# A planned RWKV block on one core: the landing times in the planner made later, and the turns of all pieces of work listed anew

## The chip, the cores and the metric

The kernel runs on one core of a Trainium2 chip. The metric is the device time of one execution in microseconds (us); lower is better. The kernel before was timed three times: 614.04, 616.27 and 617.69 us, with a median of 616.27 us.

## What is computed

The reference is one RWKV block with eight sequences of 256 tokens, 512 channels and 32 heads of 16 channels. Cut to what matters:

```python
xn = ln(x, ln1_w, ln1_b);  sx = token_shift(xn, state[:, 1])
xxx = tanh((xn + sx * maa_x) @ maa_w1).reshape(b, l, 5, 1, 32)
x5 = xn[:, :, None] + sx[:, :, None] * (maa_stack + matmul(xxx, maa_w2))
w = exp(-exp(time_decay + tanh(x5[:, :, 1] @ decay_w1) @ decay_w2))
r, k, v = x5[3] @ Wr.T, x5[0] @ Wk.T, x5[2] @ Wv.T
g = silu(x5[4] @ Wg.T)
# for every token t, with s a 16x16 state per head:
#   a = k_t v_t^T;  out_t = r_t (u * a + s);  s = a + w_t * s
att = group_norm(outs) * gn_w + gn_b
x = x + att * g @ Wo.T
xn2 = ln(x, ln2_w, ln2_b);  sx2 = token_shift(xn2, state[:, 0])
rr = sigmoid((xn2 + sx2 * ffn_maa_r) @ ffn_Wr.T)
kk = square(relu((xn2 + sx2 * ffn_maa_k) @ ffn_Wk.T))
x = x + rr * (kk @ ffn_Wv.T)
```

Everything is in 32-bit floats.

## The kernel before

**Stages.** The work of each of the eight sequences ("batches" b = 0 to 7) is cut into three stages: `inputs_of_scan` (first norm, token shift, the five mixes, the projections k, v, r, g and the decay w), `scan` (the recurrence), and `rest` (group norm, output projection Wo, second norm, and the feed-forward part with the weights Wfk, Wfr and Wfv). Constants and the weights Wk, Wr, Wg and Wv stay in SBUF. Wo, Wfk, Wfr and Wfv are loaded again for each batch, each in two halves of 512 KB, into a pool of four tiles called `Ws`. At any time the stages of three neighbouring batches overlap: the rest of one, the scan of the next, the inputs of the one after.

**The scan.** A batch has four channel blocks of four row groups, so 16 pieces of scan for a batch and 128 in all. For each piece v must stand repeated over 16 rows. To get that, v is first written to a DRAM tile `vo` by a DMA of ScalarE's queue, and then read back by a DMA of SyncE's queue that broadcasts it into a tile `vs` of 512 KB (six such tiles). A broadcast for batch b, block and row group is called vs*b*_*block*_*group* below. When it has landed, a small ScalarE copy (L944) sets the start value, a VectorE multiply (L951, in six pieces a GpSimd one, L948) brings in k, VectorE scans (L953), GpSimd multiplies by r (L956), and TensorE sums over the rows (L964).

**The planner.** No piece is issued where it is written. Each call adds a piece of work (`Op`) to a `Plan`: its engine, a cost, the tiles it writes and reads. There are 2648 pieces: 400 of TensorE, 490 of VectorE, 1102 of ScalarE, 405 of GpSimd, 251 DMAs of SyncE's queue. `TURNS` gives each piece a number from 0 to 2647, its turn, in 25 rows: one for the constants and one for each of the 24 stages, and within a row in the order in which the pieces were added. `order` then takes again and again, of the pieces whose inputs have all been placed, the one with the lowest turn, gives it a start in a calendar of its own, and puts it off if no tile of a pool that it needs is free. So the turns fix the order of the instructions on each engine, and on SyncE's queue the order of the DMAs. That queue works in order: a DMA whose tile is not yet free holds up all DMAs behind it.

**The landing times.** In that calendar a transfer lands `WAY` (1.4 us) plus a wire time after its start, and its user may start a further lag later. Both numbers come from `LANDS`, by the name of the tile; what has no entry gets (KB / 308, 1.7). Transfers also share the wire: one lands no sooner than the one before it plus its own wire time. The calendar has one more effect on the program: where several tiles of a pool are free, a piece gets the one that by the calendar came free last. Nothing else of the calendar is in the program; engines and queues wait for semaphores alone.

Of the kernel before, what the change touches and what calls it, by code (L numbers as in the profile page):

```python
# [68 lines left out]
class Plan:  # L69
# [5 lines left out]
    LANDS = {"vs__": (2.3, 1.45), "rsb_": (0.5, 0.5), "sq_": (0.5, 0.5), "s": (0.3, 1.4), "vo_": (0.7, 1.4), "vo__": (0.35, 1.4),  # L75
             "o_": (0.7, 1.2), "x": (1.8, 1.3), "xt": (1.7, 1.3), "xs": (0.7, 0.9), "idt": (0.2, 1.6)}
# [43 lines left out]
    def stage(self):  # L120
# [1072 lines left out]
```

## Time and profile before

| | |
|---|---|
| median of three timed runs | 616.27 us |
| the profiled execution's own time | 617.54 us |
| its span, first to last instruction | 615.8 us |
| median issue to landing: broadcasts `vs`, 128 of them | 5.8 us |
| the same: Wo, Wfk, Wfr, Wfv halves, 16 each | 5.8, 7.0, 5.9, 5.0 us |
| the same: x for the residual, x for the first norm | 6.3, 6.1 us |
| the same: state, v written to DRAM, output | 5.1, 5.1, 4.6 us |
| ScalarE table loads | 36 of 1.28 us |

The profiled execution took 1.3 us more than the median of the timed runs. In the profile PE is TensorE's matmuls, PEld its weight loads, DVE VectorE, ACT ScalarE, POOL GpSimd, SP SyncE. "L951" is line 951 of the kernel. A wait "DVE vs L951 <- DMA vs<-vo" is time in which VectorE stood idle before an instruction of line 951 that writes a `vs` tile, until a DMA from `vo` to `vs` had landed. The matmuls of this kernel all have line 432, 826, 964 or a few others, since a helper issues them. Ends of matmuls are modelled, so that a busy PE is not a PE at its peak.

### The profile page before, as it was taken

The numbers are of one execution on the slowest core, as the hardware profiler recorded it, in microseconds if no ns is written. First come the engines' busy times: TensorE is split into PE (matmuls) and PEld (weight loads), VectorE is DVE, ScalarE is ACT, GpSimd is POOL, SyncE is SP. The second block draws the span as 40 slices with busy tenths as digits, with TensorE's granted clock in tenths as the row PEclk, the third lists the DMA queues.
The fourth block names the chain that finished last, engine by engine and source line by source line (L and its number), as shares of the span: only waits on it lengthen the run. The fifth ranks groups of instructions, "written<-read, shape, count | busy, mean of one in ns | idle before, by whom it ended". The sixth has DMA issues, their size and how long they took to land.

```text
span 615.8 us, 17481 instructions
## 1 busy us (share of the span) xinstructions
PE 599.6 (97%) x7246; PEld 349.9 (57%) x7246; DVE 543.5 (88%) x492; ACT 508.5 (83%) x1166; POOL 520.1 (84%) x417
## 2 busy tenths in 40 slices
PE   8999999899999999998999999999999999999987
PEld 7575555467544864376553674455644564556464
DVE  5799899999999997898989998999999999995342
ACT  5988689989999999976999888998988789955341
POOL 2899999999999998998879997999979997987030
PEclk9999999999999999999999999999999999999999
DMA  9798784788959677659688896876967599781632
GB/s 310 217 251 224 205 199 140 201 212 224 243 145 264 162 200 218 179 155 246 183 240 247 221 255 166 213 187 172 259 180 229 134 267 255 208 228 32 224 124 81
DMA packets 52639, 124.76 MB, mean 203 GB/s; under 512 B 5840, under 2 KB 11344, under 8 KB 52560
## 3 DMA queue, kind: packets, MB, share of 16 engines
q1 hardware_dynamic: 48048, 119.39, 70.3%
q10 hardware_dynamic: 4512, 4.26, 2.2%
q8 instruction: 57, 0.93, 0.7%
q14 instruction: 22, 0.18, 0.1%
HBM read 115.25 MB, written 8.39 MB: 201 GB/s over the span
## 4 chain that ended last, share of the span: by engine, by line
PE 56%; POOL 15%; ACT 14%; DVE 5%; DMA 5%; issue 4%; ACTq 0%; DVEq 0%; POOLq 0%
PE ps L432 46%; POOL st L956 8%; DMA vs<-vo 5%; PE ps L964 5%; POOL mix L786 2%; PE ps L644 2%; PE ps L826 2%; POOL mix L700 2%; ACT L1117 1%; DVE st L953 1%; ACT mix L698 1%; ACT sq L1023 1%; ACT ps L768 1%; ACT wrep L932 1%; PE ps L555 1%
## 5 line engine op out<-in xcount | busy, mean ns | idle before, releaser
L953 DVE TENSOR_TENSOR_SCAN st<-wrep,vs 128x1024 f32<-128x1024 f32 x128 | 288.9, 2278 | 4.6 <-PE ps L964 1.1
L956 POOL TENSOR_TENSOR st<-st,r 128x1024 f32<-128x1024 f32 x128 | 254.5, 2004 | 10.9 <-DVE st L953 10.7
L951 DVE TENSOR_TENSOR vs<-vs,ps 128x1020 f32<-128x1020 f32 x122 | 143.0, 1203 | 8.4 <-DMA vs<-vo 7.8
L432 PE MATMUL ps<-Ws,mix 128*32 128x512 f32 (+3 forms) x872 | 115.7, 586 | 0.4 <-DVE o L1084 0.2
L432 PEld LDWEIGHTS ps<-Ws,mix 128*32 128x32 f32 (+1 forms) x872 | 38.4, 116 | 62.7 <-issue 52.1
L700 POOL TENSOR_TENSOR mix<-mix,xn 128x512 f32<-128x512 f32 x44 | 47.7, 1099 | 29.1 <-DVE mix L693 22.8
L786 POOL TENSOR_TENSOR mix<-mix,xn 128x512 f32<-128x512 f32 x62 | 66.9, 1098 | 6.1 <-DVE mix L770 5.8
L964 PE MATMUL ps<-st,con 128*32 128x256 f32 x1024 | 62.6, 380 | 0.5 <-POOL st L956 0.3
L432 PE MATMUL ps<-mix,Wv 128*32 128x256 f32 (+1 forms) x856 | 59.8, 379 | 1.5 <-DVE mix L783 1.0
L432 PE MATMUL ps<-mix,Wg 128*32 128x256 f32 (+1 forms) x664 | 58.6, 380 | 2.6 <-ACT w L849 1.7
L432 PE MATMUL ps<-mix,Wr 128*32 128x256 f32 (+1 forms) x832 | 59.2, 380 | 0.0
L432 PE MATMUL ps<-mix,Wk 128*32 128x256 f32 (+1 forms) x760 | 59.0, 379 | 0.0
L432 PE MATMUL ps<-mix,Ws 128*32 128x256 f32 (+1 forms) x664 | 57.5, 379 | 1.4 <-DVE mix L693 1.4
L432 PE MATMUL ps<-Ws,g 128*32 128x512 f32 (+1 forms) x416 | 57.1, 593 | 1.5 <-POOL g L1035 1.5
L912 ACT COPY att<-ps 32x256 f32<-32x256 f32 x128 | 46.6, 364 | 4.9 <-PE ps L904 1.6
L432 PEld LDWEIGHTS ps<-mix,Wg 128*32 128x32 f32 (+1 forms) x664 | 40.5, 124 | 17.6 <-issue 2.5
L768 ACT ACTIVATE ps<-ps,vec 128x256 f32<-128x256 f32 x112 | 46.6, 444 | 4.3 <-PE ps L432 3.0
L432 PEld LDWEIGHTS ps<-mix,Ws 128*32 128x32 f32 (+1 forms) x664 | 40.0, 124 | 17.2 <-DVE mix L693 1.8
L432 PEld LDWEIGHTS ps<-mix,Wv 128*32 128x32 f32 (+1 forms) x856 | 38.6, 115 | 18.7 <-DVE mix L783 1.4
L432 PEld LDWEIGHTS ps<-mix,Wk 128*32 128x32 f32 (+1 forms) x760 | 39.3, 119 | 17.4 <-issue 1.5
L964 PEld LDWEIGHTS ps<-st,con 128*32 128x32 f32 x1024 | 33.2, 110 | 28.0 <-issue 5.1
L432 PEld LDWEIGHTS ps<-mix,Wr 128*32 128x32 f32 (+1 forms) x832 | 36.7, 116 | 19.5 <-issue 2.0
(134 smaller groups left out, 962.4 us busy)
## 6 DMA issues: line engine op xcount, KB each, us to landing
vs<-vo SPq DMA_DIRECT2D x128, 512.0 KB, 5.8
Ws<-in_wo SPq DMA_DIRECT2D x16, 512.0 KB, 5.8
Ws<-in_fk SPq DMA_DIRECT2D x16, 512.0 KB, 7.0
Ws<-in_fr SPq DMA_DIRECT2D x16, 512.0 KB, 5.9
Ws<-in_fv SPq DMA_DIRECT2D x16, 512.0 KB, 5.0
x<-in_x SPq DMA_DIRECT2D x9, 512.0 KB, 6.3
vo<-v ACTq DMA_DIRECT2D x15, 256.0 KB, 5.1
out<-o SPq DMA_DIRECT2D x15, 256.0 KB, 4.6
```

The source lines that it names most:

```text
L432: nc.tensor.matmul(out[i : i + n], lhsT=w[:, i : i + n], rhs=x, start=first, stop=final)
L555: nc.tensor.matmul(ps()[:, 0, :], lhsT=warm[:, 0, 0:P], rhs=warm[:, 0, 0:T], start=True, stop=True)
L644: nc.tensor.transpose(to[:, m, n * P : (n + 1) * P], xh[n]()[:, k * P : (k + 1) * P], idt())
L700: gp(512, t, [t, xn[q]], lambda q=q, t=t: nc.gpsimd.tensor_tensor(t(), t(), xn[q]()[:, :, 1 : T + 1], ALU.add))
L768: act(256, p_, [p_, vec], lambda g=g, q=q, m=m, p_=p_: nc.scalar.activation(p_()[:, m, :], p_()[:, m, :], AF.Identity, bias=col(f"maa_{g}" ...
L786: gp(512, t, [t, xn[q]], lambda q=q, t=t: nc.gpsimd.tensor_tensor(t(), t(), xn[q]()[:, :, 1 : T + 1], ALU.add))
L826: nc.tensor.matmul(pd()[i : i + 32, 0, :], lhsT=w, rhs=src[k // 2]()[:, k % 2, :], start=(k == begin), stop=(k == end))
L912: act(350, atts[q], [pc], lambda i=32 * (2 * q + m), m=m, q=q, h=32 * h: nc.scalar.copy(atts[q]()[h : h + 32, m, :], pc()[i : i + 32, 0, :]))
L951: dve(4 * T, [vs], [vs, kp], lambda m=m, vs=vs, kp=kp: nc.vector.tensor_tensor(vs()[:, :, 1:T], vs()[:, :, 1:T], kp()[:, m : m + 1, 1:T].t ...
L953: dve(4 * T, [st], [w, vs, first], lambda w=w, vs=vs, st=st: nc.vector.tensor_tensor_scan(st().rearrange("p n t -> p (n t)"), w().rearrang ...
L956: gp(4 * T, st, [st, r], lambda m=m, st=st, r=r: nc.gpsimd.tensor_tensor(st(), st(), r()[:, m : m + 1, :].to_broadcast([P, 4, T]), ALU.mul ...
L964: nc.tensor.matmul(pat()[32 * i : 32 * i + 32, 0, :], lhsT=con()[:, s : s + 32], rhs=done[i]()[:, j, :], start=(j == 0), stop=(j == 3),)
```

## The change

It does two things. In `LANDS` the second number (the lag) of most transfers grows, and the four streamed weights get entries of their own:

```diff
-    LANDS = {"vs__": (2.3, 1.45), "rsb_": (0.5, 0.5), "sq_": (0.5, 0.5), "s": (0.3, 1.4), "vo_": (0.7, 1.4), "vo__": (0.35, 1.4),
-             "o_": (0.7, 1.2), "x": (1.8, 1.3), "xt": (1.7, 1.3), "xs": (0.7, 0.9), "idt": (0.2, 1.6)}
+    LANDS = {"vs__": (2.3, 2.45), "s": (0.3, 2.4), "vo_": (0.7, 2.2), "vo__": (0.35, 2.0), "o_": (0.7, 1.2), "x": (1.8, 2.3),
+             "xt": (1.7, 2.0), "xs": (0.7, 0.9), "idt": (0.2, 1.6), "Wfk_": (1.7, 2.7), "Wfr_": (1.7, 2.7),
+             "Wfv_": (1.7, 2.7), "Wo_": (1.7, 2.7)}
```

No DMA of this kernel has a tile named `rsb` or `sq` first, so the two entries that go meant nothing. And all 25 rows of `TURNS` are new:

```diff
     TURNS = """
-        8 74 18 43 53 81 61 64 90 79 102 99 173 150 5 33 118 145 151 146 24 15 34 26 47 49 31 46 56 30 35 48 32
-        44 60,
...
+        14 20 12 17 19 82 83 21 23 93 134 116 107 106 3 35 110 121 146 168 9 10 13 49 50 51 34 56 61 48 53 54 47
+        55 59,
...
```

The first row shows how such a row is read. Its places 11 and 12 are the two halves of Wr (from 102 and 99 to 134 and 116), places 13 and 14 those of Wg (from 173 and 150 to 107 and 106). Read in the same way, some DMAs that are spoken of below, with their turns before and after, and in brackets how many turns their first user comes behind them:

| DMA | before | after |
|---|---|---|
| vs0_2_3 | 286 (1) | 275 (14) |
| vs0_2_1 | 308 (1) | 271 (38) |
| xt3 and x20, x for later stages | 279, 266 | 410, 313 |
| vs4_0_1 | 1308 (25) | 1320 (32) |
| vs4_0_3 | 1328 (29) | 1304 (8) |
| vs4_0_2 | 1345 (13) | 1324 (38) |
| Wfr2, the two halves | 1267, 1317 | 1263, 1276 |
| Wfk2, the two halves | 1306, 1356 | 1307, 1225 |
| vs5_0_3 | 1696 (1) | 1613 (41) |
| vs5_1_2 | 1651 (32) | 1732 (1) |
| x25, x for a later stage | 1666 | 2100 |
| Wfk4, one half | 2020 | 1780 |
| vs0_0_2 and vs0_0_1, the first broadcasts | 112, 114 | 145, 149 |

Over the 128 broadcasts the middle number in brackets goes from 26 to 38 turns, and that of the lowest quarter from 9 to 24. Below 15 turns are 43 broadcasts before and 15 after; below 5 turns 22 and 7.

The pieces, their costs, the engines they run on and the pools of tiles stay. What depends on the order alone changes with it: by the order of its pieces ScalarE switches its table 35 times in place of 36.

252 rows, old and new, of the table TURNS are left out of this document.

## The prediction

> **What bounds the kernel now.** I read the page's busy shares first, then the windows along the span, then who waited for a DMA, and last the queue's own order at the places found. The first part of the page (engine, busy time, share, instructions):
>
> ```profile
> span 615.8 us, 17481 instructions
> PE 599.6 (97%) x7246; PEld 349.9 (57%) x7246; DVE 543.5 (88%) x492; ACT 508.5 (83%) x1166; POOL 520.1 (84%) x417
> ```
>
> TensorE is busy 97%, so at first sight only 615.8 - 599.6 = 16.2 us can be had from any new order. The windows tell where those 16.2 us lie (stretch, its length, then each engine's busy time and instructions, granted clock, DMA share, GB/s):
>
> ```profile
> 0.00:40.00 40.00, 37.05 (x318) 28.52 (x318) 27.93 (x53) 29.50 (x71) 26.34 (x40) 1.00 0.84 259
> 40.00:120.00 80.00, 75.17 (x1320) 44.67 (x1320) 76.44 (x64) 68.59 (x151) 77.73 (x54) 1.00 0.76 197
> 120.00:280.00 160.00, 159.69 (x1804) 93.20 (x1800) 153.11 (x125) 149.25 (x356) 152.55 (x120) 1.00 0.75 200
> 280.00:320.00 40.00, 38.08 (x503) 22.42 (x507) 34.69 (x26) 34.79 (x80) 32.87 (x27) 1.00 0.83 225
> 320.00:360.00 40.00, 39.95 (x512) 21.08 (x508) 38.10 (x34) 36.14 (x92) 37.28 (x34) 1.00 0.83 230
> 360.00:400.00 40.00, 39.42 (x472) 21.09 (x464) 37.91 (x33) 34.17 (x82) 36.50 (x29) 1.00 0.80 216
> 400.00:560.00 160.00, 159.40 (x2102) 90.89 (x2095) 155.35 (x127) 137.19 (x309) 145.92 (x110) 1.00 0.74 204
> 560.00:616.00 56.00, 50.86 (x252) 28.02 (x250) 19.94 (x36) 18.84 (x32) 10.86 (x10) 0.99 0.37 127
> ```
>
> TensorE's idle time is 2.95 us in the first 40 us, 4.83 in 40 to 120, 0.31 in the long stretch to 280, 1.92 in 280 to 320, 0.05, then 0.58 in 360 to 400, 0.60 in 400 to 560, and 5.14 in the tail. The clock is full throughout. So the steady part, 40 to 560, holds 8.3 us of idle time, and it comes in lumps: long stretches have none. In 280 to 320 all four engines sag together (POOL 32.87 of 40, where it has 37.28 in the next 40 us). When all engines sag at once, what they wait for is none of them. The waits that a DMA ended, by window:
>
> ```profile
> DVE vs L951 <- DMA vs<-vo: 2.3, 1, 2.3
> POOL vs L948 <- DMA vs<-vo: 2.3, 1, 2.3
> ACT vs L944 <- DMA vs<-vo: 1.2, 1, 1.2
> ...
> DVE vs L951 <- DMA vs<-vo: 3.2, 3, 1.7
> ACT vs L944 <- DMA vs<-vo: 3.7, 1, 3.7
> ...
> DVE vs L951 <- DMA vs<-vo: 1.4, 1, 1.4
> ACT vs L944 <- DMA vs<-vo: 1.8, 2, 1.5
> ```
>
> The first three lines are the waits of 48 to 66 us, the next two of 278 to 302, the last two of 350 to 386 (total us, times, longest). Over the whole span:
>
> ```profile
> DVE vs L951 <- DMA vs<-vo: 7.8, 6, 2.3
> ACT vs L944 <- DMA vs<-vo: 7.6, 6, 3.7
> POOL vs L948 <- DMA vs<-vo: 2.3, 1, 2.3
> SPq L421 <- PE ps L432: 86.8, 29, 16.1
> ```
>
> So nearly all lateness of the broadcasts (15.9 of 17.7 us) sits in three knots. No wait of TensorE for a DMA stands in the profile: streamed weights are in time now. The chain that ended last runs through the same knots, each time over one slow broadcast:
>
> ```profile
> 51.88 10.55 DMA vs<-vo
> ...
> 281.41 10.40 DMA vs<-vo
> ...
> 361.52 11.43 DMA vs<-vo
> ```
>
> A broadcast usually lands in 5.8 us, in the knots in 10 to 11:
>
> ```profile
> DMA to landing us min/median/max: 4.2/5.8/11.8
> ```
>
> The old calendar gave it 1.4 + 2.3 + 1.45 = 5.15 us, less than that median; the new one gives 6.15.
>
> **The change part by part.**
>
> *The lags.* These numbers are no instructions. They act through the order, and through which free tile a piece takes. A broadcast is now planned for 6.15 us (measured 5.8), a weight half for 5.8 in place of 4.8 (measured 5.0 to 7.0), x for 5.5 in place of 4.5 (6.3), the state for 4.1 in place of 3.1 (5.1). All move towards the measured ones. None covers the 10 to 11 us of a knot, so the knots go only if the order takes the crowd away, or if loads are issued much sooner.
>
> At this place a rule speaks against the change. The Trainium skill, page "DMA: Bandwidth & Descriptors", section "Anatomy of one DMA — SWDGE (gpsimd) path", fits a DMA at 2.0 us plus its bytes over 436 GB/s, which for 512 KB is 3.2 us (an estimate). By it the old 5.15 us was ample, and later landings buy nothing. The trace disagrees: its fastest broadcast took 4.2 us, its median 5.8.
>
> *The order: what it does at the three knots.* 2648 turns in 615.8 us are 0.233 us each, which makes turns comparable with landings (an estimate: turns are an order, not a clock). In the table of turns the middle broadcast stands 38 turns = 8.8 us ahead of its user (before: 26 = 6.0), the lowest quarter 24 = 5.6 us (before: 9 = 2.1). The queue's issues in the second knot (start, length):
>
> ```profile
> 277.17 1.32 SPq L421 DMA_DIRECT2D vs<-vo  x2
> 278.54 0.58 SPq L421 DMA_DIRECT2D Ws<-in_fk  x1
> 279.17 0.46 SPq L421 DMA_DIRECT2D out<-o  x1
> 281.41 0.52 SPq L421 DMA_DIRECT2D vs<-vo  x1
> 281.98 0.61 SPq L421 DMA_DIRECT2D Ws<-in_fr  x1
> 284.58 3.66 SPq L421 DMA_DIRECT2D vs<-vo  x2
> 288.29 1.50 SPq L421 DMA_DIRECT2D Ws<-in_fk  x1
> ```
>
> Three weight halves and an output go in among the broadcasts of batch 4. After the change one half of Wfk2 (1356 to 1225) and one of Wfr2 (1317 to 1276) stand ahead of vs4_0_0 (1297): 1 MB leaves the crowd, 4.7 us of transfer at the 225 GB/s of that window. In the first knot x20 and xt3, again 1 MB, are moved behind the two broadcasts that came late, and these get 38 and 14 turns in place of 1 and 1. In the third knot x25 goes far back and vs5_0_3 gets 41 turns for 1, but vs5_1_2 falls from 32 turns to 1: there I count on nothing.
>
> What the first two knots cost has two ends. From above: the longest wait of one engine in each, 2.3 + 3.7 = 6.0 us, if what was lost there was never made up. From below: TensorE's own idle time there, since a stall that TensorE never feels costs little:
>
> ```profile
> 48.00:66.00 18.00, 16.69 (x309) 9.75 (x308) 15.65 (x13) 13.99 (x31) 15.73 (x13) 1.00 0.89 232
> 278.00:302.00 24.00, 22.27 (x263) 15.37 (x265) 20.23 (x17) 19.32 (x45) 19.91 (x17) 1.00 0.88 231
> 350.00:386.00 36.00, 35.60 (x432) 21.48 (x431) 33.26 (x28) 31.14 (x79) 31.42 (x25) 1.00 0.80 212
> ```
>
> That is 18 - 16.69 = 1.31 and 24 - 22.27 = 1.73, together 3.0 us. VectorE and GpSimd are nearly full too and can't make up all of it, so I take the middle: **-4.5 us**. The third knot would be worth 0.4 to 1.8 more; new short loads (below) may cost as much; 0.
>
> *New short loads.* After the change seven broadcasts have fewer than 5 turns (vs3_3_1, vs3_3_3, vs4_3_3, vs5_1_2, vs5_1_3, vs5_3_3, vs6_3_0); before, 22 had, and the waits outside the knots were 1.8 us in all. Between 0 and three waits of the usual 17.7 / 13 = 1.4 us; beside the third knot, 0.
>
> *The start.* Wg's two halves now stand ahead of Wr and of the first broadcasts. VectorE's rows there:
>
> ```profile
> 28.27 1.66 DVE L812 SCALAR_TENSOR_TENSOR mix<-ps,vec,sx 128x256 f32<-128x256 f32 x4 [4.04 <-PE ps L432]
> 29.85 1.22 DVE L951 TENSOR_TENSOR vs<-vs,ps 128x1020 f32<-128x1020 f32 x1
> ...
> 23.22 2.54 SPq L421 DMA_DIRECT2D vs<-vo  x4
> ```
>
> The first broadcast is issued at 23.22 and used at 29.85; with the shortest landing of 4.2 us it has up to 2.4 us to spare, and what covers it is VectorE's wait for TensorE until 28.27. The 1 MB of Wg takes 4.0 us at that window's 259 GB/s. So the cost lies between 0 and 4.0 - 2.4 = 1.6 us; with part of the 1 MB moved before the broadcast can be issued at all, I take **+0.5 us**. It comes back partly: later broadcasts find no Wg in their way.
>
> *The rest.* One table load of 1.28 us less, on an engine with 17% idle: 0. TensorE's order moves by 0.9 places of 400 on average, so its work and its tail (5.14 us idle, last sums, then norm and feed-forward of batch 7 one after the other) stay: 0, with 1 us to either side.
>
> *Sum.* -4.5 + 0.5 = -4.0 us. The profiled execution's 617.54 becomes 613.5. It stood 1.27 us above the median of 616.27; against the median the forecast is **612.3 us**.
>
> **The rivals.**
>
> *More than idle time is won* (606 to 609 us). Busy PE time hides waits:
>
> ```profile
> L964 PE MATMUL ps<-st,con 128*32 128x256 f32 x1024 | 62.6, 380 | 0.5 <-POOL st L956 0.3
> ```
>
> These 1024 are 32 groups of 32, which is 1.96 us a group, while groups in the chain of waits take 1.73:
>
> ```profile
> 336.88 1.73 PE ps L964 x32
> ```
>
> So 7 us of this line alone is waiting inside busy time. All three knots (7.8 us) gone and a little of this gives 616.27 - 8 to - 10. The Trainium skill, "Perfetto Trace Analysis", section "Identifying the Most-Contended Engine", says that matmul busy share is no measure of headroom and weight-load busy share (here 57%) is a better one; by it the 16.2 us is no ceiling. Against it: in 160-us stretches TensorE idles 0.3 to 0.6 us, and the changed order hardly touches it.
>
> *The lateness moves* (615 to 618 us). The DMA engines are busy 0.72 to 0.88 along the steady part, the same bytes must pass, and six `vs` and four `Ws` tiles limit how early a load can go. Then new knots form elsewhere, as vs5_1_2 and vs5_1_3 hint. No gain, 616.27 - 1 + 0.5.
>
> *The queue in order holds broadcasts up* (slower, 620 to 623 us). SyncE's queue stood 86.8 us in 29 waits of 3.0 us on average for TensorE's matmuls, mostly to free a weight tile, and all behind it stands too. Now one half of Wfk4 is 240 turns earlier (56 us): it pins one of four `Ws` tiles, and the next weights must wait at the head of the queue. A broadcast behind such a wait has 8.8 - 5.8 = 3.0 us to spare in the middle; from there on each longer wait is felt by VectorE. Three such of 3 us beyond the spare with no knot won, less what TensorE makes up, give 616.27 + 4 to + 7. Against it: broadcasts have more turns to spare than before.
>
> **How the numbers follow.** The forecast (608.5 to 614.5) has a chance of 0.45, more won 0.12, lateness that moves 0.26, the held queue 0.17. A measurement of this kernel can tell about 0.5%, 3.1 us. Under 613.2 lies all of the second case and most of the first: faster 0.50. Slower than 619.3 are the last case and a little of the third: 0.19. Between, 0.31. Leaving out about a tenth at each end gives 606 to 620 us, which holds the bounds of the knots (3.0 to 7.8), of the start and of the tail.
>
> **What would show it right or wrong.** Right: DMA waits of lines 951, 944 and 948 fall from 17.7 to under 10 us; the windows 48 to 66 and 278 to 302 show PE within 0.7 us of full; first scan no later than 32.3 us (before 31.75). Wrong: the same sum of DMA waits at other places; a PE wait for a weight transfer, which doesn't exist now; SyncE waiting over 100 us for line 432; a first scan at 33 us or later; PE idle in 120 to 280 or 400 to 560 above 2 us.

## The result, and the profile after

| | before | after |
|---|---|---|
| median of four timed runs each, us | 616.22 | 608.30 |
| lowest and highest, us | 614.04, 617.69 | 607.54, 610.79 |
| the profiled execution, us | 617.54 | 610.79 |

The ratio after to before is 0.9881, with a 95% interval of 0.984 to 0.9922: faster by 1.2%, that is 4.8 to 9.9 us. The forecast was 612.3 us in a range of 606 to 620. The direction and the range held; the gain came out 1.7 to 2 times as large as the 4.0 us that were forecast. The profiled execution of after is the slowest of its four; e2 below has the same turns, and its profiled execution took 608.69 us.

All lines of the changed kernel are one higher: L951 of before is L952 of after, L432 is L433. The first part of the page after (engine, busy time, share, instructions):

```profile
span 609.0 us, 17328 instructions
PE 597.1 (98%) x7174; PEld 349.0 (57%) x7174; DVE 540.4 (89%) x492; ACT 505.2 (83%) x1165; POOL 519.7 (85%) x417
```

TensorE's idle time is 609.0 - 597.1 = 11.9 us; it was 16.2. So 4.3 us of the 6.8 us by which the span fell are idle time, and 2.5 us are busy time of the same matmuls (roughly: the two traces hold 7246 and 7174 of their records, so some are missing in either). The windows of after, the same stretches as before (stretch, length, busy time of PE, PEld, DVE, ACT, POOL with instructions, clock, DMA share, GB/s):

```profile
0.00:40.00 40.00, 37.02 (x322) 28.41 (x326) 25.81 (x52) 29.47 (x73) 25.66 (x40) 1.00 0.88 271
40.00:120.00 80.00, 77.19 (x1336) 43.97 (x1332) 79.49 (x68) 69.22 (x154) 80.00 (x55) 1.00 0.75 197
120.00:280.00 160.00, 159.00 (x2008) 91.39 (x2004) 152.52 (x124) 149.54 (x360) 152.09 (x122) 1.00 0.79 210
280.00:320.00 40.00, 39.97 (x502) 23.18 (x496) 36.70 (x31) 36.86 (x82) 35.99 (x26) 1.00 0.75 205
320.00:360.00 40.00, 40.00 (x398) 24.72 (x391) 38.01 (x31) 34.75 (x86) 36.94 (x33) 1.00 0.83 216
360.00:400.00 40.00, 39.87 (x531) 21.76 (x533) 38.95 (x36) 36.16 (x88) 38.95 (x32) 1.00 0.85 230
400.00:560.00 160.00, 158.64 (x1911) 90.85 (x1904) 152.11 (x125) 130.86 (x297) 145.38 (x110) 1.00 0.73 198
560.00:609.00 49.00, 45.37 (x200) 24.69 (x192) 16.84 (x32) 18.34 (x32) 4.64 (x5) 1.00 0.42 140
```

TensorE's idle time went from 4.83 to 2.81 us in 40 to 120, from 1.92 to 0.03 in 280 to 320, from 0.58 to 0.13 in 360 to 400 and from 5.14 to 3.63 in the tail. It grew from 0.31 to 1.00 in 120 to 280 and from 0.60 to 1.36 in 400 to 560. GpSimd is now full for 80.00 of 80 us in 40 to 120. The waits of the whole span that a DMA ended, and the queue's wait for TensorE (total us, times, longest):

```profile
ACT vs L945 <- DMA vs<-vo: 7.6, 8, 1.7
DVE vs L952 <- DMA vs<-vo: 3.7, 2, 3.4
PE ps L433 <- DMA Ws<-in_wo: 1.0, 1, 1.0
SPq L422 <- PE ps L433: 98.0, 29, 7.9
```

VectorE waits 3.7 us for broadcasts in place of 7.8, and 3.4 of it is one wait for the very first broadcast; GpSimd's 2.3 us are gone; ScalarE's sum is the same, but in eight short waits of at most 1.7 us. In 48 to 66 and in 278 to 302 us no wait for a broadcast is left at all, and in 350 to 386 only 1.7 us of ScalarE's. New is one wait of TensorE for a half of Wo.

The scans follow one another through the whole kernel, so their ends serve as a clock for a comparison. The first and the last scan of before (start, length):

```profile
31.75 2.29 DVE L953 TENSOR_TENSOR_SCAN st<-wrep,vs 128x1024 f32<-128x1024 f32 x1 [0.68 <-ACT vs L944]
...
557.78 2.27 DVE L953 TENSOR_TENSOR_SCAN st<-wrep,vs 128x1024 f32<-128x1024 f32 x1
```

and of after (the last row holds three):

```profile
33.01 2.29 DVE L954 TENSOR_TENSOR_SCAN st<-wrep,vs 128x1024 f32<-128x1024 f32 x1
...
548.40 6.64 DVE L954 TENSOR_TENSOR_SCAN st<-wrep,vs 128x1024 f32<-128x1024 f32 x3
```

The first scan comes 1.3 us later, the last one ends 560.05 - 555.04 = 5.0 us sooner. With the last scan of each batch between them, the profiled executions differ from before's like this (us; the last column is the end of the span; the kernels e6 to e12 come below):

| | first scan | b0 | b1 | b2 | b3 | b4 | b5 | b6 | b7 | end |
|---|---|---|---|---|---|---|---|---|---|---|
| after | +1.3 | -2.3 | -4.0 | -2.7 | -1.8 | -4.1 | -5.9 | -4.9 | -5.0 | -6.8 |
| e6 | -0.7 | -1.5 | -1.5 | -1.5 | -1.6 | -3.7 | -4.1 | -4.5 | -4.5 | -4.4 |
| e7 | 0 | +1.2 | +0.7 | +0.7 | +0.7 | -0.7 | -1.4 | -2.0 | -2.0 | -3.6 |
| e8 | -0.8 | -2.1 | -3.1 | -1.8 | -0.9 | -3.3 | -4.8 | -3.8 | -3.9 | -5.6 |
| e9 | -0.7 | -3.0 | -4.9 | -3.6 | -3.3 | -5.6 | -7.4 | -8.0 | -8.1 | -9.9 |
| e10 | +0.2 | -3.4 | -4.9 | -3.5 | -2.6 | -4.9 | -6.7 | -7.3 | -7.4 | -7.5 |
| e11 | +0.2 | -3.1 | -4.1 | -2.8 | +9.7 | +7.1 | +6.0 | +5.4 | +5.7 | +5.7 |
| e12 | -0.8 | -0.1 | -0.1 | -0.1 | +2.5 | +0.2 | -1.6 | -2.2 | -2.3 | -4.1 |

In the row of after the gain comes in four large steps: 3.6 us from the first scan to the end of batch 0, 2.3 in batch 4, 1.8 in batch 5, and 1.8 behind the last scan. (Another 1.7 in batch 1 is lost again in batches 2 and 3.) These rows compare single executions. The order of e7 is before's own up to the last few us, and yet its row wanders between +1.2 and -2.0: steps under 2 us in one such row prove nothing, and the experiments were made to tell which of them are real.

Behind the last scan the changed kernel does something that the prediction had not seen. VectorE's four pieces of the feed-forward mix of batch 7 in before (shortest, median and longest in ns), then in time with GpSimd's two adds and with the matmuls that use them:

```profile
L693 DVE SCALAR_TENSOR_TENSOR mix<-sx,vec,xn x4: 480/894/1317, 588.5 to 590.6; 128x256 f32<-128x256 f32 x4
...
588.53 3.34 DVE L693 SCALAR_TENSOR_TENSOR mix<-sx,vec,xn 128x256 f32<-128x256 f32 x4
589.09 2.50 POOL L700 TENSOR_TENSOR mix<-mix,xn 128x512 f32<-128x512 f32 x2 [22.76 <-DVE mix L693]
...
591.93 6.74 PE L432 MATMUL ps<-mix,Ws 128*128 128x256 f32 x30 [1.44 <-DVE mix L693]
```

and in after:

```profile
L694 DVE SCALAR_TENSOR_TENSOR mix<-sx,vec,xn 128x256 f32<-128x256 f32 x4 | 1.7, 477 | 0.0
...
583.49 1.67 DVE L694 SCALAR_TENSOR_TENSOR mix<-sx,vec,xn 128x256 f32<-128x256 f32 x4
585.06 1.09 POOL L701 TENSOR_TENSOR mix<-mix,xn 128x512 f32<-128x512 f32 x1 [24.69 <-ACT mix L699]
```

The four pieces took 896 ns on average while GpSimd's adds ran beside them (480 ns for each of the first two, 1.31 us for each of the last two), and 477 ns when GpSimd began only as they ended. In before TensorE stands idle for 1.44 us until they are done; in after it doesn't wait for them. So here the difference, 3.34 - 1.67 = 1.67 us, is on the path to the end. What sets it is ScalarE's order of the four pieces of `xr7` that feed the adds: in before both of the second half come first, so that the first add starts early; in after the halves take turns.

### The profile page after: what moved, and what is told of

It is laid out like the page before. It is cut to its first block, busy times and chain, and to the rows that moved or that the text cites. A ratio compares the mean times of both kernels' runs of the same rounds, so it can differ in the third digit from the quotient of the medians.

```text
span 609.0 us, 17328 instructions
## 1 busy us (share of the span) xinstructions
PE 597.1 (98%) x7174; PEld 349.0 (57%) x7174; DVE 540.4 (89%) x492; ACT 505.2 (83%) x1165; POOL 519.7 (85%) x417
## 4 chain that ended last, share of the span: by engine, by line
PE 75%; POOL 15%; DMA 4%; ACT 2%; issue 2%; DVE 2%; ACTq 0%; SPq 0%; DVEq 0%; POOLq 0%
PE ps L433 62%; POOL st L957 7%; PE ps L965 7%; POOL mix L787 4%; PE ps L645 2%; DMA Ws<-in_wo 2%; PE ps L827 1%; POOL vs L949 1%; DMA vs<-vo 1%; PE ps L556 1%; DMA vo<-v 1%; ACT att L1031 1%; POOL att L1027 1%; PE ps L991 1%; POOL rk L900 1%
## 5 line engine op out<-in xcount | busy, mean ns | idle before, releaser
L952 DVE TENSOR_TENSOR vs<-vs,ps 128x1020 f32<-128x1020 f32 x122 | 142.5, 1199 | 3.7 <-DMA vs<-vo 3.7
L433 PE MATMUL ps<-Ws,mix 128*32 128x512 f32 (+3 forms) x872 | 115.5, 585 | 0.1
L433 PEld LDWEIGHTS ps<-Ws,mix 128*32 128x32 f32 (+1 forms) x872 | 38.4, 116 | 62.6 <-issue 56.5
L433 PE MATMUL ps<-mix,Wv 128*32 128x256 f32 (+1 forms) x832 | 59.4, 379 | 1.3 <-DVE mix L784 1.3
L433 PE MATMUL ps<-Ws,g 128*32 128x512 f32 (+1 forms) x416 | 57.0, 593 | 3.1 <-POOL g L1036 2.1
L433 PE MATMUL ps<-mix,Wr 128*32 128x256 f32 (+1 forms) x760 | 59.3, 380 | 0.0
L433 PE MATMUL ps<-mix,Wk 128*32 128x256 f32 (+1 forms) x808 | 58.4, 379 | 0.4 <-DVE mix L771 0.4
L433 PE MATMUL ps<-mix,Wg 128*32 128x256 f32 (+1 forms) x616 | 58.6, 380 | 0.1
L433 PE MATMUL ps<-mix,Ws 128*32 128x256 f32 (+1 forms) x688 | 58.3, 379 | 0.0
L433 PEld LDWEIGHTS ps<-mix,Wv 128*32 128x32 f32 (+1 forms) x832 | 37.9, 116 | 19.8 <-DVE mix L784 1.7
L433 PEld LDWEIGHTS ps<-mix,Wg 128*32 128x32 f32 (+1 forms) x616 | 40.7, 128 | 14.6 <-DVE vs L952 0.6
L433 PEld LDWEIGHTS ps<-mix,Ws 128*32 128x32 f32 (+1 forms) x688 | 39.9, 123 | 15.9 <-issue 0.5
L433 PEld LDWEIGHTS ps<-mix,Wr 128*32 128x32 f32 (+1 forms) x760 | 38.2, 119 | 18.5 <-issue 2.6
L433 PEld LDWEIGHTS ps<-mix,Wk 128*32 128x32 f32 (+1 forms) x808 | 37.8, 117 | 18.7 <-issue 1.5
```

The source lines that it names most:

```text
L433: nc.tensor.matmul(out[i : i + n], lhsT=w[:, i : i + n], rhs=x, start=first, stop=final)
L952: dve(4 * T, [vs], [vs, kp], lambda m=m, vs=vs, kp=kp: nc.vector.tensor_tensor(vs()[:, :, 1:T], vs()[:, :, 1:T], kp()[:, m : m + 1, 1:T].t ...
```

## The experiments

Where turns are edited, they are shown by the name of the piece. Each ratio is that of timed runs to runs of before on the same chip (medians of before 614.3 us beside e1 to e4, 614.98 beside e5 to e8, 614.94 beside e9 to e12).

### The landing numbers alone, and the turns alone

e1 is before with the new landing numbers, e2 is after with the old ones:

```diff
 e1, on before
-    LANDS = {"vs__": (2.3, 1.45), "rsb_": (0.5, 0.5), "sq_": (0.5, 0.5), "s": (0.3, 1.4), "vo_": (0.7, 1.4), "vo__": (0.35, 1.4),
+    LANDS = {"vs__": (2.3, 2.45), "s": (0.3, 2.4), "vo_": (0.7, 2.2), "vo__": (0.35, 2.0), "o_": (0.7, 1.2), "x": (1.8, 2.3),
...
 e2, on after
-    LANDS = {"vs__": (2.3, 2.45), "s": (0.3, 2.4), "vo_": (0.7, 2.2), "vo__": (0.35, 2.0), "o_": (0.7, 1.2), "x": (1.8, 2.3),
+    LANDS = {"vs__": (2.3, 1.45), "rsb_": (0.5, 0.5), "sq_": (0.5, 0.5), "s": (0.3, 1.4), "vo_": (0.7, 1.4), "vo__": (0.35, 1.4),
...
```

> Before with the new LANDS and the old TURNS: the order on every engine stays, only the choice among free tiles can differ. Theory Q (the order of the DMAs in SyncE's queue made the gain): 616 us within 2, the waits of L951, L944 and L948 for broadcasts stay near 17.7 us. Rival T (the tiles that the later calendar picks made it): 608 to 612 us.

> After with the old LANDS and the new TURNS: the new order with the old choice of tiles. Theory Q and theory E (the order on the computing engines made the gain): 608 us within 2. Rival T: 612 us or more, since the tiles are then picked by the earlier landings and loads wait for tiles that are freed later.

e1 took 614.92 us, a ratio of 1.0002 [0.9978, 1.0027]; e2 took 608.59 us, 0.989 [0.9858, 0.9923]. The landing numbers, and with them which of several free tiles a piece takes, do nothing that can be measured. The whole gain is in the order.

### The order of the DMAs alone, and of the engines alone

e3 is before with the new turns on all DMAs and none of the engines' work; e4 is after with the old turns on all DMAs:

```diff
 e3, on before: pieces of SyncE's queue, and ScalarE's writes of v
-turns of before
+turns of after
 e4, on after: the same pieces
-turns of after
+turns of before
```

> Before with the new LANDS, and of the new TURNS only those of the DMAs (SyncE's and the writes of vo on ScalarE's queue); all other pieces keep their old turns. Theory Q: 609 to 612 us, the knots at 48 to 66 and 278 to 302 us gone from the waits, first scan at about 33 us as in the changed kernel. Theory E: 615 us or more.

> After, but the DMAs (SyncE's and the writes of vo) with their old turns; the computing engines with the new ones. Theory Q: 614 to 617 us less 1.5 us for the shorter tail, with late broadcasts above 12 us of waits again. Theory E: 608 to 611 us.

Both missed by far: e3 took 686.43 us, 1.1153 [1.1104, 1.1202], e4 678.47 us, 1.1006 [1.0961, 1.1051]. Neither half of the change can stand without the other, so this split can't say which of them holds the gain. The waits of e3 show what it costs when the two orders don't fit:

```profile
ACT vs L945 <- DMA vs<-vo: 69.4, 20, 9.0
DVE vs L952 <- DMA vs<-vo: 33.7, 13, 9.6
...
SPq L422 <- ACT vs L945: 12.9, 1, 12.9
```

Those of e4 are alike, 84.9 us in 30 waits. In both, broadcasts come late by up to 9.6 and 7.7 us at a time, because they stand in a queue in order behind a transfer whose tile isn't free yet: in e3 the head of the queue once waits 12.9 us for a tile that ScalarE has still to use. This is the rival of the held queue, at a price of 64 to 72 us. Not all of it is waiting: TensorE's granted clock, full in before and after, was 0.97 on average in these two, and what that part costs was not measured. The changed kernel doesn't pay it, since its two orders were made together.

### The second knot alone

e5 is before with the one shift that the prediction had counted on between 278 and 302 us, two weight halves (1 MB) ahead of the broadcasts of batch 4:

```diff
-Wfk2, one half 1356
-Wfr2, one half 1317
+Wfk2, one half 1225
+Wfr2, one half 1276
```

> Before with two turns changed: one half of Wfk2 (1356 to 1225) and one of Wfr2 (1317 to 1276), as in the changed kernel; so 1 MB is issued before the first broadcasts of batch 4. Theory Q: the DMA waits between 278 and 302 us (6.9 us) fall under 2, the last scan of batch 4 ends 2 to 3 us sooner than 361 us, and the kernel takes 2 to 3 us less, ratio 0.995 to 0.997. Rival E (the compute order of that place made its gain): waits move by under 2 us, ratio 0.999 to 1.002.

It took 615.39 us, 0.9997 [0.998, 1.0015]: nothing. The waits of e5 in 278 to 302 us:

```profile
ACT vs L944 <- DMA vs<-vo: 2.6, 1, 2.6
DVE vs L951 <- DMA vs<-vo: 0.6, 1, 0.6
```

These 3.2 us look like half of before's 6.9. But e7 has before's order at this place, unchanged, and shows (its lines are 28 higher)

```profile
DVE vs L979 <- DMA vs<-vo: 1.9, 2, 1.0
ACT vs L972 <- DMA vs<-vo: 0.8, 1, 0.8
```

2.7 us, while e1, also with before's order, shows

```profile
DVE vs L952 <- DMA vs<-vo: 3.6, 3, 1.6
ACT vs L945 <- DMA vs<-vo: 2.6, 1, 2.6
```

6.2 us. In e6 below, whose changes lie 200 us further ahead, it is 2.0 us:

```profile
DVE vs L951 <- DMA vs<-vo: 1.1, 2, 0.8
ACT vs L944 <- DMA vs<-vo: 0.9, 1, 0.9
```

So the knot of the old order is of no fixed size: 2.0 to 6.9 us from one execution to the next, and the profile that the prediction was made from had the largest. With the new order it is gone, and not by luck: after, e2, e8, e9, e10 and e12, six executions, have no wait there. What does away with it is more than these two halves, or something else; which turns do it was not isolated.

### The first knot alone

e6 is before with four turns of after: x20 and xt3 later, the two late broadcasts earlier.

```diff
-x20 266, xt3 279
-vs0_2_1 308, vs0_2_3 286
+x20 313, xt3 410
+vs0_2_1 271, vs0_2_3 275
```

> Before with four turns changed: x20 and xt3 later (266 to 313, 279 to 410), vs0_2_1 and vs0_2_3 sooner (308 to 271, 286 to 275), as in the changed kernel. Theory Q: the DMA waits between 48 and 66 us (5.8 us on three engines) fall under 1, the last scan of batch 0 ends 2 to 4 us sooner than 93.0 us, ratio 0.994 to 0.998. Rival E: batch 0 ends within 1 us of before, ratio 0.999 to 1.002.

It took 613.69 us, 0.9978 [0.9959, 0.9996], so -1.4 us, of which the interval can tell little more than the sign. The waits of e6 in 48 to 66 us fall from 5.8 to 1.7:

```profile
POOL vs L948 <- DMA vs<-vo: 1.4, 1, 1.4
DVE vs L951 <- DMA vs<-vo: 0.3, 1, 0.3
```

and the window of e6:

```profile
48.00:66.00 18.00, 17.52 (x328) 10.16 (x324) 17.68 (x15) 14.76 (x34) 16.56 (x13) 1.00 0.83 208
```

TensorE has 0.48 us idle there in place of 1.31, and VectorE is busy for 17.68 us in place of 15.65. Batch 0 ends 1.5 us sooner, and that stays to the end of batch 3 without a loss. Both fall short of what was expected of e6 (waits under 1 us, batch 0 ending 2 to 4 us sooner). This knot too is of no fixed size: with the old order the same waits were 5.8 us in before, 6.1 in e7, 8.2 in e12, 8.8 in e1 and 10.7 in e5, and here the profile that the prediction was made from had the smallest. The mechanism is the one that was forecast for this knot, and by the timed runs its size too.

### The tail

e7 is before, with ScalarE's pieces of `xr7` that came early put a little later, the halves taking turns as in after; e10 is after with the order of before there (turns between two others are written with a decimal).

```diff
 e7, on before: xr7, first half (two pieces, add), second half (two pieces, add)
-2609 2610 2611, 2601 2604 2605
+2609 2610.6 2611, 2609.5 2610.9 2611.2
 e10, on after: the same pieces
-2604 2606 2607, 2605 2609 2619
+2606 2606.5 2607, 2603.5 2603.6 2603.7
```

> Before with six turns of the last stage changed: ScalarE's four pieces of xr7 (L698) go behind its o6_1 and in the order 0, 1, 0, 1, so that GpSimd's adds (L700) come after VectorE's four xk7 pieces (L693) and not beside them. Theory G (GpSimd beside VectorE doubled those pieces, 896 ns in place of 477): L693 falls under 520 ns, TensorE's wait of 1.4 us for it is gone, the span from the last L964 to the end is 1.3 to 1.8 us shorter, ratio 0.997. Rival: the pieces stay near 900 ns, the tail stays.

> After with ScalarE's four pieces of xr7 back in the order 1, 1, 0, 0, so that GpSimd's first add starts beside VectorE's xk7 pieces again. Theory G (GpSimd beside VectorE doubles those pieces): their mean rises from 477 ns to 700 or more, the span from the last sum over rows to the end grows from 49.6 to 50.5 to 51.5 us, the kernel is 1 to 2.5 us slower than the changed one, ratio to before 0.990 to 0.993. Rival (the shorter tail has another cause, as the table load that went): within 0.5 us of the changed kernel, 0.988.

e7 took 612.38 us, 0.9954 [0.9935, 0.9973]; e10 took 610.37 us, 0.9924 [0.9904, 0.9943]. The pieces of e7, with the adds:

```profile
586.56 1.67 DVE L721 SCALAR_TENSOR_TENSOR mix<-sx,vec,xn 128x256 f32<-128x256 f32 x4
588.13 2.14 POOL L728 TENSOR_TENSOR mix<-mix,xn 128x512 f32<-128x512 f32 x2 [23.78 <-ACT mix L726]
```

and of e10:

```profile
581.10 3.34 DVE L722 SCALAR_TENSOR_TENSOR mix<-sx,vec,xn 128x256 f32<-128x256 f32 x4
581.65 2.50 POOL L729 TENSOR_TENSOR mix<-mix,xn 128x512 f32<-128x512 f32 x2 [23.67 <-DVE mix L722]
```

It goes both ways: 1.67 us for the four pieces where the add comes behind them, 3.34 where it runs beside them. Without the early add e7 gains 1.6 us behind the last scan (-2.0 to -3.6 in the table); with it e10 gains nothing there (-7.4 to -7.5), where after gained 1.8. By the timed runs it is 0.46% in e7, 2.8 us, and 0.34% between e10 and e2, 2.1 us. The profiles of all these kernels agree: from the end of the last scan to the end of the span it is 55.6 to 55.7 us where the add is early (before, e1, e5, e6, e10, e11) and 54.0 to 54.1 where it isn't (after, e2, e7, e8, e9, e12). So about 2 us of the gain are here, in the turns of six pieces (four of ScalarE, two adds of GpSimd), which have nothing to do with landings.

### The start

In after Wg's two halves go ahead of Wr and of the first broadcasts. e8 puts them back where before has them; e9 puts them behind the sixth broadcast.

```diff
 on after, the two halves of Wg
-107 106
+173 150
...
-107 106
+232.2 232.1
```

> After with the two halves of Wg back at their old turns (107 to 173, 106 to 150), behind the first broadcasts. Theory S (Wg ahead of them cost the 1.3 us by which the first scan is later): the first write of vo lands in under 3 us in place of 5.2, the first scan starts at 31.5 to 32 us in place of 33.0, and the kernel is 0.5 to 1.5 us faster than the changed one, about 607 us. Rival: the first scan moves, but the end does not (POOL and PE are the bound to 120 us and make it up), 608 to 609 us; or Wg late makes the g projection wait, 609 us or more.

> After with both halves of Wg behind vs0_1_1, the sixth broadcast, instead of ahead of the first: nothing is then in the way of the first write of vo, of the second, or of the six broadcasts. Theory P (from the first scan to about 117 us GpSimd is the bound, so the end follows the time at which it has its first scan, if no broadcast makes it wait later): first scan at 31 to 31.7 us (33.0 in the changed kernel), no wait of L949's line for a DMA, the kernel 1 to 2 us faster than the changed one, 606 to 607.5 us, ratio to before 0.985 to 0.988. Rival (the order after the start absorbs it): 608 to 610 us.

First what happens in after, on its chain of waits (start, length):

```profile
20.22 5.20 DMA vo<-v
...
25.44 6.16 DMA vs<-vo
```

The first write of v, 128 KB, is issued at 20.22 us and takes 5.20 us; only then can the first broadcast be issued, and VectorE waits for it until 31.69. In before the same write was issued at 21.50 and the broadcast at 23.22, 1.72 us later. SyncE's queue had issued Wg at 12.40 and Wr at 14.42 in after, and Wr's halves took 9.2 to 9.6 us to land. The windows of the two writes, after's first and then before's:

```profile
20.00:25.40 5.40, 5.40 (x98) 2.91 (x96) 2.75 (x6) 4.65 (x14) 5.40 (x6) 1.00 0.64 234
```

```profile
21.50:23.20 1.70, 1.70 (x38) 1.01 (x34) 1.70 (x6) 1.52 (x6) 1.70 (x3) 1.00 0.23 77
```

The DMA engines were busy 0.64 of the time and moved 234 GB/s while the write was under way in after, 0.23 and 77 GB/s in before. The Trainium skill, page "DMA: Bandwidth & Descriptors", section "Issuing engines are not separate DMA queues", says that the DMAs of all engines run on the same 16 DMA engines and interleave. The trace agrees: the write is on ScalarE's queue, the weights on SyncE's, and beside them it took three times as long. Without Wg ahead of it, in e8 and e9, it took 2.65 and 2.35 us.

With Wg late, e8 starts its first scan at 30.96 us, 2.1 sooner than after, and yet it took 610.58 us, 0.9928 [0.99, 0.9956], no gain over after's order in e2 (0.989). Its chain of waits shows why:

```profile
25.46 8.15 DMA vo<-v
...
33.63 8.43 DMA vs<-vo
```

and its waits in 20 to 60 us (L977 is after's L949):

```profile
POOL vs L977 <- DMA vs<-vo: 2.0, 1, 2.0
```

The second write of v takes 8.15 us, the fifth broadcast behind it 8.43 (in after the write was issued at 25.81 and the fifth broadcast at 31.87, 6.06 later), and GpSimd stands still for 2.0 us. GpSimd can't afford it: in after it is busy without a gap from 40 to 120 us. The slow write is not the work of Wg: in e9, where Wg is issued nearly 10 us behind it, it took 8.45 us, and in before 9.00. In these three it comes behind four broadcasts, in after behind one. What Wg delays in e8 is the fifth broadcast: with Wg later, in e9, that took 4.53 us in place of 8.43, and GpSimd doesn't wait. e9 has the shortest span of the profiled executions (605.9 us, and a first scan at 31.09), but its timed median is 608.69 us, 0.9896 [0.9876, 0.9916]. Beside e2's 608.59 that is no difference: the rival of its expectation held, not theory P.

### Half of the new order

e11 has the new turns up to 1000, and then the old; e12 the old up to 1000, and then the new.

```diff
 e11: turn of a piece
+a if a < 1000 else 5000 + b
 e12
+b if b < 1000 else 5000 + a
```

Here a is a piece's turn in after and b that in before.

> The new turns for the pieces with a new turn below 1000 (to about 230 us), and behind them the rest in the old turns. Theory A (the gain is a sum of places): start and first knot as in the changed kernel, later knots and tail as before: last scan of batch 2 some 2.5 us sooner than before and that kept to the end, 612 to 613 us against 615, ratio 0.994 to 0.998. Rival W (a list is good only as a whole, as with the DMA turns alone): waits for broadcasts behind the seam, 617 us or more.

> The old turns for the pieces with an old turn below 1000, and behind them the rest in the new turns. Theory A: the first knot as before, the second and third gone, the tail short: last scan of batch 3 as before, last scan of batch 7 some 2 to 3 us sooner, the end 4 to 5 us sooner, 610 to 611 us against 615, ratio 0.991 to 0.995. Rival W: waits behind the seam, 617 us or more.

e11 took 623.27 us, 1.0133 [1.0111, 1.0155], e12 613.87 us, 0.9984 [0.9969, 0.9999]. Both are slower than theory A had them (612 to 613 and 610 to 611 us). At the seam, 200 to 278 us, the two orders don't meet. e11 waits there

```profile
ACT vs L945 <- DMA vs<-vo: 12.6, 2, 6.7
```

and loses 12.5 us between the ends of batches 2 and 3 (-2.8 to +9.7). e12 waits

```profile
DVE vs L952 <- DMA vs<-vo: 4.7, 2, 3.1
ACT vs L945 <- DMA vs<-vo: 3.6, 1, 3.6
```

and loses 2.6 there. Beside the seams the halves do what the whole does: e11 has gained 2.8 us by the end of batch 2 (after 2.7), e12 gains 4.8 from the end of batch 3 to that of batch 7 (after 3.2) and 1.8 behind it. But a seam that costs 2.6 to 12.5 us can also move waits out of the stretch behind it, so these two sizes are bounds at best.

## Why the prediction was right in its direction and too small in its size

**The lags do nothing by themselves.** Right: 1.0002 in e1. The order was the change.

**Where the gain lies.** Three profiled executions have before's order up to the tail (before, e1, e7) and three have after's (after, e2, e10). The first scan, then how long each batch takes from the end of the one before it, and what is behind the last scan (there e10 counts with before and e7 with after), in us:

| | first scan | b0 | b1 | b2 | b3 | b4 | b5 | b6 | b7 | behind |
|---|---|---|---|---|---|---|---|---|---|---|
| old order | 31.1-31.8 | 61.4-62.9 | 59.9-60.4 | 64.5 | 72.1 | 69.9-71.7 | 69.4-70.2 | 67.6-68.2 | 60.2-60.5 | 55.6-55.7 |
| new order | 32.0-33.0 | 57.9 | 58.8-58.9 | 65.8 | 73.0-73.2 | 69.0 | 68.3 | 67.6-69.2 | 60.1 | 54.0-54.1 |
| mean, new less old | +0.9 | -4.5 | -1.3 | +1.3 | +1.0 | -2.0 | -1.4 | +0.3 | -0.2 | -1.7 |

**The first knot.** Right in mechanism and size. Its bounds were 1.3 (TensorE's idle time) and 2.3 us (the longest wait); e6 gives 1.4 us, nearer to the lower end, with an interval from 0.2 to 2.5.

**The second knot.** The step that failed is "1 MB leaves the crowd". Moving that megabyte alone gives 0.9997. And the 1.7 to 3.7 us that the step was to bring back were read off one execution in which the knot was at its largest of those seen; some other executions of the same order have less than half of it. The new order does clear the place, in every one of six executions, and batch 4 takes 0.9 to 2.7 us less with it, 2.0 in the mean of three. That is near the size that was counted on, but not by the cause that was named for it, so it was luck. (In e11, behind its seam, batch 4 took no more than 68.7 us in the old order.)

**The third knot and the steady part behind it, counted at 0.** Batch 5 takes 1.1 to 1.9 us less with the new order, though waits for broadcasts in 350 to 386 us remain (1.3 to 1.7 us in after, e2 and e10; 1.5 to 3.2 in before, e1 and e7). That was in the margin the prediction had named, 0.4 to 1.8, and left out. Which turns do it was not tested.

**The first four batches, beyond the first knot.** The prediction had nothing here. Batches 0 and 1 take 5.8 us less in the mean, of which e6's four turns can explain 0.8 to 2.3 in batch 0 (60.6 us in e6), and batches 2 and 3 take 2.3 more. In part this is work put off: from the first scan to the end of batch 0 GpSimd is busy for 59.0 to 59.8 us in the old order and 57.1 to 57.3 in the new.

**The start.** The bound was right, 0 to +1.6 us: the first scan came 1.3 us later in after, 0.9 in the mean of the table. The sign that went with it was wrong: a first scan at 33 us or later was to mean that the change had gone wrong, and it came at 33.01 (at 32.30 in e2 and 31.97 in e10, with the same turns there). What decides is not the first scan alone but whether GpSimd runs without a gap from there to the end of batch 0. GpSimd in before, for 60 to 80 us,

```profile
60.00:80.00 20.00, 18.69 (x332) 10.55 (x320) 17.63 (x17) 13.82 (x31) 17.73 (x13) 1.00 0.86 217
```

lost 2.3 us, and in after

```profile
60.00:80.00 20.00, 20.00 (x364) 11.96 (x360) 19.90 (x18) 14.67 (x34) 20.00 (x14) 1.00 0.79 205
```

none. e8 and e9 put the first scan 2 us forward of after's, and gain nothing by it in the timed runs: from there to the end of batch 0 they take 60.1 and 59.1 us, after, e2 and e10 57.9.

**The rest and the tail, counted at 0 with 1 us to either side.** This is the other step that failed. It reasoned that TensorE's order hardly moves and that its work in the tail therefore stays. But the tail is set by what runs beside what on VectorE and GpSimd, and there the turns of six pieces are worth about 2 us. The trace of before held the evidence: TensorE's wait of 1.44 us for four pieces of 896 ns on average, where pieces of the same size elsewhere took half of that (L812, a row that the prediction shows: four in 1.66 us).

**The signs.** The two windows are full, as foretold (18.00 - 17.92 and 24.00 - 24.00 us idle):

```profile
48.00:66.00 18.00, 17.92 (x328) 10.69 (x332) 17.90 (x15) 15.67 (x38) 18.00 (x13) 1.00 0.83 213
278.00:302.00 24.00, 24.00 (x272) 15.78 (x272) 23.55 (x20) 21.41 (x49) 23.17 (x17) 1.00 0.79 198
```

The waits for broadcasts fell from 17.7 to 11.3 us, not under 10 (9.7 in e2, 7.0 in e10); 7.6 of these are ScalarE's, an engine that is busy 83%, in waits of at most 1.7 us. A wait of TensorE for a weight appeared, which was to mean that the change had gone wrong; it is one wait of 1.0 us for a half of Wo. SyncE's queue waited 98.0 us for TensorE, under the 100 that were to mean trouble, and TensorE's idle time in 120 to 280 and 400 to 560 us, 1.00 and 1.36, stayed under 2.

**The sum.** Forecast -4.0; by the timed runs -6.8 us (e2's 1.1% of 614.3) to -7.9. Single edits account for 1.4 at the first knot and 2.1 to 2.8 in the tail (1.7 by the profiles). The other 3 us or so were not isolated by an edit. The table puts 3.4 us in batches 4 and 5, where the second and third knots lie, and about 1 us in the start and the first four batches beyond e6's 1.4; its columns add up to about -7.5 us. Of the rivals, "more than idle time is won" (606 to 609 us) was nearest in time. Its reason fits in part only: of the 6.8 us by which the span fell, 4.3 are idle time, and no more than the rough 2.5 us of busy time are what it spoke of; and it had looked for them in the knots, not in the tail.

## What to carry to other kernels

A wait in one profile is a sample: before a forecast is built on its size, look for the same wait in other executions of the same order, since here one knot ranged from 2.0 to 6.9 us and another from 5.8 to 10.7. An order of engines and an order of a DMA queue belong together, and a part of one taken from elsewhere can cost ten times what the whole gains. And in a tail where few engines work, compare the duration of each instruction with that of its like elsewhere: what runs beside it may be its price.

## What the runs showed of the hardware

- VectorE and GpSimd slow each other on one pair of operations and not on another. The scalar-tensor-tensor operation on 128x256 floats, with `sx` and `xn` both in SBUF, took 477 to 478 ns in after and e7 and 894 to 896 ns on average in before and e10, with a GpSimd add beside it; the two adds took 2.50 us in place of 2.14. By single instructions the first two of the four pieces lost nothing; each of the last two took 1.31 us and ended 0.28 us behind the end of one of the adds. So they look held up until an add was done, and not run at half speed. The Trainium skill, page "SBUF — State Buffer", section "Who interferes with whom", says that a VectorE instruction with two inputs in SBUF contends with a GpSimd instruction that reads SBUF, and calls the contention for the ports that they share an exclusive lock. The trace agrees that they contend, and the ends fit a lock; that it is the ports, no run here shows. Not the whole of an instruction is shut out: one after the other they take 1.67 + 2.14 = 3.81 us, side by side both were done in 591.87 - 588.53 = 3.34 us. The scans have one of their inputs in PSUM; their lengths were 2220 to 2292 ns for all 128, though GpSimd was at work beside most of them.
- A 128 KB write of v, otherwise alike, took 1.72 us before and 5.20 us after, with weights from another queue under way. The second such write took 9.00 us in before, 8.15 in e8 and 8.45 in e9, behind four broadcasts, and 6.05 in after, behind one.
- A stall can cost TensorE more than its own length. In the first knot of e1 it stood idle for 4.00 - 1.84 = 2.16 us, and its granted clock in the next 4 us was 0.57 (stretch, length, busy times, clock, DMA share, GB/s):

```profile
62.00:66.00 4.00, 1.84 (x36) 0.93 (x32) 1.09 (x1) 1.60 (x5) 3.26 (x3) 1.00 1.02 236
66.00:70.00 4.00, 4.00 (x48) 2.08 (x44) 4.00 (x5) 3.40 (x10) 4.00 (x3) 0.57 0.37 112
```

In e5 it was 2.52 us and 0.59. In before, e7 and e12 it stood idle for 1.31, 1.43 and 2.03 us at this place, and the clock in 66 to 70 us was 1.00. So part of what this knot costs in some executions of the old order may be a slow clock behind it; how much was not measured.

- Executions of one order differ at a single place, the second knot, by 5 us in its waits (2.0 to 6.9). The whole time of before went from 612.87 to 618.31 us in 29 runs on one chip.
